# Where the degree sums of a graph kernel are made, and how far the weighing of values lags behind the scores

## The chip, the core and the metric

One Trainium2 chip, of which the kernel uses one core. The metric is the device time of one execution in microseconds (us); it was 10797.06 us, the median of three runs between 10793.86 and 10804.12. The core has five engines with a queue of instructions each, which each works through in order: TensorE (PE, matrix products), VectorE (DVE), ScalarE (ACT), GpSimdE (POOL) and SyncE (SP, which issues the DMA transfers here). They wait for each other by semaphores.

## What is computed

Four graph layers on 3327 nodes with 128 features and a dense 0/1 adjacency matrix `adj` of 3327 x 3327. Each layer takes `h = relu(layernorm(x))` and adds its result to `x`. Two of the layers matter here. Layer 1 is attention with the adjacency matrix as a bias on every score; it has 128 small heads of width 8 and takes most of the time:

```
q = (x @ Wq.T).reshape(d, n, h)          # d = 128 heads, n = 3327 nodes, h = 8
k = (x @ Wk.T).reshape(d, n, h)
v = (x @ Wv.T).reshape(d, n, h)
a = einsum('dnh,dmh->dnm', q, k) * scale
a = softmax(a + adj + adj, axis=2)
out = einsum('dnm,dmh->dnh', a, v)
```

Layer 3 needs the degree of every node, `jnp.sum(A, axis=-1)`, for its scaling by `1/sqrt(degree)`.

## The kernel before

**Stages.** Layer 0 and the projections of layer 1 take the first 416 us. Then comes the attention, to about 10070 us, and then the end: the output projection of layer 1 and layers 2 and 3. Up to the end of the attention the instructions stand on each engine in the order in which the program writes them (`manual_schedule`); nothing reorders them.

**Loops of the attention.** The 3327 queries are cut into seven chunks of 476 (`q_chunks`, the last of 471). Within a chunk the 128 heads are taken in 32 groups of four, and within a group the 3327 keys in 26 key tiles of 128. Key tiles are handled in blocks: in chunk 0 a block is a pair of key tiles (`PAIRS`, 13 blocks to a group), in chunks 1 to 6 mostly three (`TRIPLES`). For every key tile and head there are 128 x 476 scores. They come in two ways:

- *early* scores: PE multiplies keys by queries into a PSUM bank (L911, tile `early`), DVE adds the adjacency tile on the way to SBUF (L927, tile `p_early`), and when the whole block has been added, ACT takes one exp of all of it (L932). In chunk 0 a block has five early heads: the four of its first tile and one of its second. Each is a product and an add of its own, into single banks of which there are four (`bufs=4`).
- *late* scores, three heads of the block's last tile: PE puts them into one three-bank PSUM tile of which there is a single one (`late`), for one or two of the heads adds the adjacency with a product by `two_i` (L940), ACT takes the exp from PSUM (L941, tile `p_late`), and POOL multiplies the others by the exp of the adjacency (L943).

**Weighing.** Once a key tile's exps are there, PE weighs the values with them: four fp32 products per key tile (eight passes in the trace), one per head, into the bank `acc` (L954), which sums over the 26 key tiles of the group. After the last of them DVE copies `acc` to SBUF (L963, tile `o`, named `o4` in the code) and four DMAs store it (`ot`). The next group's first weighing starts a new sum in the same bank, so it waits for that copy. Tile sets of `p_early` and `p_late` come from a pool with four buffers, so block N takes the memory of block N-4.

**Order on PE in chunk 0.** For each block PE's instructions stand in the order "aAWlcW": `a` and `A` are the products of the four early heads of the first tile, `W` the weighing of one key tile, `l` the late products, `c` the fifth early product, and `W` the weighing of another key tile. The text calls the two weighings W1 and W2. DVE's adds stand in the order of their products: four for `a` and `A`, one for `c`. Which key tile is weighed follows from `ahead`: a `W` is carried out when

```
if n_tiles + heads / 2 >= n_weighed + ahead:
    weigh_next()
```

holds, where `n_tiles` counts the key tiles of the blocks begun before and `heads` the early heads of this block so far. Every second key tile, DVE also makes a pair of keys contiguous (`key_pair`, L656); at tile 5 of a group POOL does it (L658).

**Degree sums.** The adjacency tiles of a chunk are doubled and scaled by POOL (L285) and added up over the key tiles into `deg_half`, 128 partitions x 476 (L296), the last of them at key tile 17 of the chunk's group 0. What is left is the sum over the partitions. `store_sum` (L298) makes it: PE multiplies a column of ones by `deg_half` into one row of a PSUM bank, DVE scales that row to SBUF (L301), and a DMA stores it to `degd` (L302). For chunk 0 this is done among the projections (`r == 1`). For chunks 1 to 6 it is done in group 1 at key tile 10, in the PSUM tile `late` and the SBUF tile `o4`. Before layer 2 the sums are read back from `degd` into `deg`.

Of the kernel before, what the change touches and what calls it, by code (L numbers as in the profile page):

```python
# [8 lines left out]
F32 = mybir.dt.float32  # L9
# [11 lines left out]
P = 128  # L21
N = 3327
D = 128
T = 26
# [19 lines left out]
def chunks(width, size):  # L44
    return [(a, min(size, width - a)) for a in range(0, width, size)]
# [11 lines left out]
def kernel(  # L57
# [75 lines left out]
    def inv_sqrt(pool, src, name, scale=1.0, bias=0.0):  # L133
        r = pool.tile([P, T], F32, name=name)
        nc.scalar.activation(r, src, AF.Sqrt, bias=bias, scale=scale)
        nc.vector.reciprocal(r, r)
        return r
# [157 lines left out]
        else:  # L295
            nc.gpsimd.tensor_tensor(deg_half[:, :w], deg_half[:, :w], a2[:, :w], op=ALU.add)  # L296

    def store_sum(c, dp, row):  # L298
        q0, w = q_chunks[c]
        nc.tensor.matmul(dp[:1, :w], ones, deg_half[:, :w], start=True, stop=True)  # L300
        nc.vector.tensor_scalar_mul(row[:1, :w], dp[:1, :w], 0.5 / S_SCALE)  # L301
        nc.sync.dma_start(degd[:, q0 : q0 + w], row[:1, :w])  # L302

    def node_quad(agg, ps, y, t0, n, scale=1.0):
        mp = ps.tile([P, 4, D], F32, name="mp")
# [476 lines left out]
    for r in range(T):  # L782
        project_rows(r, hT4[r // 4][:, r % 4, : rows_of(r)], w_st, st, ps)
        c = r // 4 + 1
        if c < len(CS):
            if r % 4 < 2:
                norm(c, r % 4)
            if r % 4 == 2:
                norm(c, 2)
        if 2 + r < len(CS):  # L790
            more_rows(2 + r)
        if 3 + r == len(CS):
            ctx_0.close()
            kq = ctx_at.enter_context(tc.tile_pool(name="at_kq", bufs=2))
            e_pool = ctx_at.enter_context(tc.tile_pool(name="at_e", bufs=T // 2 + 1))
            kq0 = ctx_at.enter_context(tc.tile_pool(name="at_kq0", bufs=1))
            side = ctx_st.enter_context(tc.tile_pool(name="l1_side", bufs=1, side="right"))
            low_rows = []
            row = side.tile([P, 1], I32, name="row")
            nc.gpsimd.iota(row, pattern=[[0, 1]], base=0, channel_multiplier=1)  # L800
            for bit in (1, 2):
                odd = side.tile([P, 1], I32, name=f"odd{bit}")
                nc.vector.tensor_scalar(odd, row, bit, None, op0=ALU.bitwise_and)
                low = side.tile([P, 1], F32, name=f"low{bit}")
                nc.vector.tensor_scalar(low, odd, -1.0 / bit, None, op0=ALU.mult)
                low_rows.append(low)
            low_k, low_q = low_rows
        if 3 + r >= len(CS):
            while len(early) > n_early * (T - 1 - r) // (T + 3 - len(CS)):
                early.pop(0)()  # L810
        if r % 2 and r // 2 < len(CS):
            store_x(r // 2)
        if r == 1:
            store_sum(0, ps.tile([P, 512], F32, name="tp"), l1.tile([1, QW], F32, name="deg_row", bufs=1))
            nc.sync.dma_start(degd[:, N:], ones[:1])

    mx = side.tile([P, 5], F32, name="mx")
    for i, m in enumerate((q_max, k_max, a_max, low_bits, x_max)):
# [38 lines left out]
    with tc.tile_pool(name="at_in", bufs=1) as a_pool, tc.tile_pool(name="at_p", bufs=4) as p_pool, tc.tile_pool(  # L857
# [38 lines left out]
        class Block:  # L896
# [48 lines left out]
            def weigh(self, pos):  # L945
                t = self.t0 + pos
                q0, w = q_chunks[self.c]
                kp = rows_of(t)
                for i in range(4):
                    if pos < self.n - 1:  # L950
                        p = self.early[:, 4 * pos + i]
                    else:
                        p = self.late[:, i] if i < 3 else self.early[:, 4 * pos]
                    nc.tensor.matmul(  # L954
                        acc[32 * i : 32 * i + EA, :w],
                        self.v4[:kp, i, t, :],
                        p[:kp, :w],
                        start=(t == 0),
                        stop=(t == T - 1),
                    )  # L960
                if t == T - 1:
                    o4 = a_pool.tile([P, QW], F32, name="o4")
                    nc.vector.tensor_copy(o4[: 96 + EA, :w], acc[: 96 + EA, :w])  # L963
                    for i in range(4):
                        n0 = (4 * self.g + i) * N + q0
                        nc.sync.dma_start(ot[:, n0 : n0 + w], o4[32 * i : 32 * i + EA, :w])

        with tc.manual_schedule(engines=engines), ExitStack() as ctx_ps:
# [21 lines left out]
            def events(c, g, t, n, a_in):  # L990
                nonlocal coming, part, ahead_part, n_stored, k_next
                more = n < len(groups)
                if t == 8 and more:
                    coming = first[n] if n < len(first) else load_rest(*groups[n])
                if c == 0:
                    if t == 0:
                        part = ahead_part
                    part.at(t)
                    if t == 20 and g + 1 < n_groups:
                        ahead_part = Parting((g + 3) % n_groups)  # L1000
                        ahead_part.load(0)
                if t == 17:
                    while to_sum:
                        add_to_sum(*to_sum.pop(0))
                if t == 10 and g == 1 and c:
                    store_sum(c, ps.tile([P, 3, 512], F32, name="late")[:, 0], a_pool.tile([P, QW], F32, name="o4"))
                if t % 2 and n_stored < len(pairs):
                    store_tile_keys(n_stored)
                    n_stored += 1
                if t % 2 and len(pairs) < n_pairs:  # L1010
                    key_pair(nc.gpsimd if t == 5 else nc.vector, k_ins, pairs)
                if t == 14 and n + 1 < n_groups:
                    k_ins.append(load_keys(groups[n + 1][1]))
                if t == 4 and n_groups <= n < len(groups):
                    k_next = load_tile_keys(groups[n][1])
                if t == 6 and c + 1 < len(q_chunks):
                    for _ in range(min(len(to_store), 1 + T // n_groups)):
                        store_adj(*to_store.pop(0))
                    a_in += [load_adj(c + 1, i) for i in range(len(a_next), T * (g + 1) // n_groups)]
                if t == T - 4 and c + 1 < len(q_chunks):  # L1020
                    for a, i, w in a_in:
                        a_next.append(doubled(adj_pools[(c + 1) % 2], a[: rows_of(i), :w], i, w))
                        to_sum.append((a_next[-1], c + 1, i == 0))
                        to_store.append((c + 1, i, a_next[-1]))

            coming = part = None
            for n, (c, g) in enumerate(groups, 1):
# [10 lines left out]
                for i, size in enumerate(TRIPLES if c else PAIRS):  # L1038
                    if c:
                        n_g, keys, order = 3, (lambda t, k=k_now: k[:, t]), ORDERS[size, n_block % 2]  # L1040
                    else:
                        n_g, order = 1 if t0 + 1 in PARTING_TILES else 2, PAIR_ORDER
                        keys = lambda t, g=g: pairs[(g * T + t) // 2][:, t % 2]
                    block = Block(c, g, t0, size, i, q4, v4, a_t, e_t[i], n_g, keys)
                    to_weigh += [(block, pos) for pos in range(size)]
                    ahead = 7 if c else 6
                    heads = 0
                    for step in order:
                        if step == "W":
                            if n_tiles + heads / 2 >= n_weighed + ahead:  # L1050
                                weigh_next()
                        elif step == "l":
                            block.late_ones()
                        else:
                            pos, which = PIECES[step] if step != "c" else (size - 1, (3,))
                            heads += len(which)
                            block.sums(pos, which, c > 0)
                    n_tiles += size
                    n_block += 1
                    for t in range(t0, t0 + size):  # L1060
                        events(c, g, t, n, a_in)
                    t0 += size
                    if g == n_groups - 1 and c + 1 < len(q_chunks):
                        while len(e_next) < len(late_tiles) and late_tiles[len(e_next)] < t0:
                            e_next.append(exp_of(a_next[late_tiles[len(e_next)]], c + 1))
# [72 lines left out]
    def tail(general):  # L1138
# [13 lines left out]
        with ExitStack() as s:  # L1152
# [30 lines left out]

            if not general:
                nc.sync.dma_start(deg, degd.rearrange("o (p t) -> (o p) t", t=T))
            d1 = inv_sqrt(pool, deg, "d1")
            d1_in, d1_out = d1, d1
            if not general:
# [399 lines left out]
```

## Time and profile before

| | |
|---|---|
| median of three runs | 10797.06 us |
| the profiled execution, its own time | 10795.13 us |
| its span in the profile | 10793.2 us |
| granted clock of PE, mean | 0.988 |
| busy: PE, DVE, ACT, POOL | 91%, 93%, 92%, 68% |
| copies of `acc` from 416 to 1892 us (chunk 0 and the first of chunk 1) | 33, the first at 476.8, the last at 1890.3 us |
| matrix product, keys by queries, 476 columns (L911) | 367 ns |
| one pass of the weighing (L954) | 566 ns |
| DVE add of one head in chunk 0 (L927, 128 x 476) | 643 ns |
| ACT exp of a pair's early scores (L932, 128 x 2380) | 2365 ns |

The durations of one instruction overlap with the next one's: adds that follow each other start 0.56 us apart. So the text reads the time of a step from the starts in the timeline and takes a duration only where something waits for its end. In the timeline a row is: start, us taken, engine, line, operation, tiles, shapes, how many were merged, and in brackets the idle time before it with what ended it. The page's "granted clock" is the share of PE's full clock that it was given in a stretch.

### The profile page before, as it was taken

How to read it: one execution, taken by the hardware profiler on the slowest of the kernel's cores; microseconds unless marked ns; L12 is line 12 of the kernel's file. 1: busy time of each engine (PE TensorE's matmuls, PEld its weight loads, DVE VectorE, ACT ScalarE, POOL GpSimd, SP SyncE). 2: the span in 40 equal slices, each digit the busy share in tenths (PEclk: the TensorE clock that was granted, in tenths of full speed). 3: DMA queues.
4: the chain of work that ended last, by engine and by line, in shares of the span. 5: the costliest groups of instructions: out<-in, count | busy, mean ns of one | idle time of the engine just before them, and what ended most of it. 6: DMA issues, size and time to landing. Idle time of an engine off the chain costs nothing. (4 is left out here: it accounts for less than half of the span.)

```text
span 10793.2 us, 183718 instructions
## 1 busy us (share of the span) xinstructions
PE 9771.8 (91%) x74212; PEld 2128.9 (20%) x74212; DVE 10091.4 (93%) x11605; ACT 9945.0 (92%) x4716; POOL 7295.1 (68%) x3314
## 2 busy tenths in 40 slices
PE   7899999999989999899999899998999989999896
PEld 3211111111111111111111111111111111111453
DVE  6799999999999999999999999999999999999666
ACT  2799999999999999999999999999999999999432
POOL 3388887777777777777777777777777766666203
PEclk9999999999999999999999999999999999999998
DMA  8644443111111111111111111111111111111422
GB/s 300 202 101 102 101 101 86 44 44 44 44 44 42 45 44 44 43 44 46 42 45 45 42 41 45 46 42 45 42 44 44 44 37 37 38 36 37 159 95 101
DMA packets 459189, 709.21 MB, mean 66 GB/s; under 512 B 53128, under 2 KB 387967, under 8 KB 452698
## 3 DMA queue, kind: packets, MB, share of 16 engines
q1 hardware_dynamic: 455144, 690.86, 21.7%
q8 instruction: 585, 9.58, 0.4%
q0 software_dynamic: 3184, 6.51, 0.2%
q14 instruction: 276, 2.26, 0.1%
HBM read 557.43 MB, written 139.73 MB: 65 GB/s over the span
## 5 line engine op out<-in xcount | busy, mean ns | idle before, releaser
L927 DVE TENSOR_TENSOR p_early<-early,a 128x952 f32<-128x952 f32 (+3 forms) x10336 | 9152.4, 956 | 207.6 <-PE early L911 178.5
L943 POOL TENSOR_TENSOR p_late<-p_late,e 128x1428 f32<-128x1428 f32 (+3 forms) x2144 | 6397.5, 2984 | 2570.9 <-ACT p_late L941 2556.0
L932 ACT ACTIVATE p_early<-p_early 128x4284 f32<-128x4284 f32 (+3 forms) x2144 | 8077.5, 3767 | 14.7 <-DVE p_early L927 14.7
L954 PE MATMUL acc<-p_early,v 128*9 128x476 f32 (+3 forms) x33728 | 5709.9, 566 | 153.6 <-issue 110.1
L941 ACT ACTIVATE p_late<-late 128x1428 f32<-128x1428 f32 (+1 forms) x2144 | 3865.4, 1803 | 43.9 <-PE late L911 17.2
L911 PE MATMUL early<-q,k_in 32*128 32x476 f16 (+1 forms) x14784 | 3060.5, 367 | 439.1 <-DVE p_early L927 416.2
L954 PE MATMUL acc<-p_late,v 128*9 128x476 f32 (+3 forms) x12864 | 2104.0, 566 | 0.3 <-POOL p_late L943 0.3
L911 PEld LDWEIGHTS <-k_in 32*128 32x128 f16 x19968 | 765.3, 91 | 5461.1 <-issue 5440.9
L911 PE MATMUL late<-q,k_in 32*128 32x476 f16 (+1 forms) x5184 | 779.0, 367 | 179.3 <-ACT p_late L941 179.1
L954 PEld LDWEIGHTS acc<-p_early,v 128*9 128x9 f32 (+1 forms) x33728 | 655.7, 88 | 1145.6 <-issue 966.8
L911 PE MATMUL early<-q,k 32*128 32x476 f16 x2080 | 389.0, 368 | 7.5 <-DVE p_early L927 6.0
L954 PEld LDWEIGHTS acc<-p_late,v 128*9 128x9 f32 (+1 forms) x12864 | 240.7, 88 | 533.1 <-issue 438.8
L911 PEld LDWEIGHTS <-k 32*128 32x128 f16 x3328 | 120.8, 91 | 784.9 <-issue 767.3
L235 PE MATMUL agg_ps<-a,part 128*128 128x512 bf16 (+1 forms) x1092 | 229.5, 371 | 4.2 <-ACT agg L1372 3.2
L656 DVE TENSOR_REDUCE k<-k_in 128x256 f16<-128x256 f16 x377 | 220.8, 586 | 0.0
L285 POOL TENSOR_SCALAR a<-a_in 128x476 bf16<-128x476 f32 (+2 forms) x156 | 219.0, 1404 | 0.5
L348 PE MATMUL agg_ps<-a,part 128*128 128x494 bf16 (+5 forms) x728 | 168.2, 390 | 54.2 <-DMA a<-in_adjT_dram 53.3
L587 POOL TENSOR_TENSOR lo<-raw,hi 96x278 f16<-96x278 f32 (+1 forms) x256 | 182.4, 713 | 20.5
L296 POOL TENSOR_TENSOR deg_half<-deg_half,a 128x476 f32<-128x476 f32 (+1 forms) x175 | 191.9, 1097 | 2.1
L194 ACT ACTIVATE agg<-agg_ps 128x512 f32<-128x512 f32 x9 | 4.7, 597 | 196.3 <-PE agg_ps L235 196.3
L940 PE MATMUL late<-a,two_i 128*128 128x476 bf16 x544 | 182.2, 373 | 0.0
L1367 PE MATMUL sp<-yT,hT 128*128 128x512 f32 (+1 forms) x364 | 171.3, 612 | 11.6 <-ACT agg L1372 5.7
(288 smaller groups left out, 2682.1 us busy)
## 6 DMA issues: line engine op xcount, KB each, us to landing
k_in<-keyd SPq DMA_DIRECT2D x192, 832.0 KB
v<-vd SPq DMA_DIRECT2D x896, 117.0 KB
a<-in_adjT_dram SPq DMA_DIRECT2D x39, 1663.5 KB
a<-adj SPq DMA_DIRECT2D x78, 831.8 KB
a_in<-in_adjT_dram SPq DMA_DIRECT2D x125, 238.0 KB
keyd<-k SPq DMA_DIRECT2D x416, 64.0 KB
k_in<-kt SPq DMA_DIRECT2D x240, 104.0 KB
q<-qt SPq DMA_DIRECT2D x1520, 14.9 KB
```

What stands on the lines that cost most here:

```text
L235: nc.tensor.matmul(acc[c][:, :w], part[:, t, :], a[:, c0 : c0 + w], start=(t == 0 and i == 0), stop=(t == T - 1 and i == len(parts) - 1),)
L285: nc.gpsimd.tensor_scalar(a2[:kp, :w], a, 2.0 * S_SCALE, None, op0=ALU.mult)
L296: nc.gpsimd.tensor_tensor(deg_half[:, :w], deg_half[:, :w], a2[:, :w], op=ALU.add)
L587: nc.gpsimd.tensor_sub(self.lo[side][:, p], raw, hi)
L656: nc.vector.tensor_reduce(k, src.unsqueeze(3), AX.X, ALU.max)
L911: return nc.tensor.matmul(sp[:, : self.we], self.keys(self.t0 + pos)[r], self.q4[r, : self.we], start=True, stop=stop)
L927: Block.first_sum = nc.vector.tensor_tensor(p, scores, a2, op=ALU.add)
L932: nc.scalar.activation(p, p, AF.Exp, scale=1.0 / S_SCALE)
L940: nc.tensor.matmul(late[:, i, :we], two_i, self.a[pos][:, :we], start=False, stop=True)
L941: nc.scalar.activation(self.late[:, :, :we], late[:, :, :we], AF.Exp, scale=1.0 / S_SCALE)
L943: nc.gpsimd.tensor_tensor(g, g, self.e[:, :we].unsqueeze(1).to_broadcast([P, self.n_g, we]), op=ALU.mult)
L954: nc.tensor.matmul(acc[32 * i : 32 * i + EA, :w], self.v4[:kp, i, t, :], p[:kp, :w], start=(t == 0), stop=(t == T - 1),)
```

## The change

It has two parts.

First, the sums over the partitions no longer go into one row. `deg_half` becomes the stationary side, 96 columns at a time, and the ones the moving side, so that each product gives a column of 96 sums. Five columns hold a chunk's sums, and they go into the columns of `acc` behind its 476. They are made in group 0 of chunks 1 to 6, after the last weighing of the group and before the copy of `acc`, which takes them along; two more DMAs store them to `degd`, element by element. For chunk 0 the same is done in a bank among the projections. The scaling by `0.5 / S_SCALE` is done once at the end on `deg`, and the node that does not exist gets a zero there and a one added afterwards.

Second, in chunk 0 `ahead` is 8 instead of 6. At the start of a block the weighing stands seven key tiles behind instead of five: W1 of block N weighs the second tile of block N-4 (before, of block N-3), and W2 the first tile of block N-3 (before, of block N-2). The copy of `acc` moves from the third block of the next group to the fourth. Chunks 1 to 6 keep their 7.

```diff
-    def store_sum(c, dp, row):
+    SUM_ROWS = 96
+
+    def sum_columns(c, acc):
+        w = q_chunks[c][1]
+        parts = chunks(w, SUM_ROWS)
+        for j, (m0, n) in enumerate(parts):
+            nc.tensor.matmul(acc[:n, QW + j : QW + j + 1], deg_half[:, m0 : m0 + n], ones, start=True, stop=True)
+        return QW + len(parts)
+
+    def store_sums(c, o):
         q0, w = q_chunks[c]
-        nc.tensor.matmul(dp[:1, :w], ones, deg_half[:, :w], start=True, stop=True)
-        nc.vector.tensor_scalar_mul(row[:1, :w], dp[:1, :w], 0.5 / S_SCALE)
-        nc.sync.dma_start(degd[:, q0 : q0 + w], row[:1, :w])
+        whole = w // SUM_ROWS
+        nc.sync.dma_start(dram(degd, q0, [[1, SUM_ROWS], [SUM_ROWS, whole]]), o[:SUM_ROWS, QW : QW + whole])
+        if w % SUM_ROWS:
+            nc.sync.dma_start(dram(degd, q0 + whole * SUM_ROWS, [[1, w % SUM_ROWS], [1, 1]]), o[: w % SUM_ROWS, QW + whole : QW + whole + 1])
...
         if r == 1:
-            store_sum(0, ps.tile([P, 512], F32, name="tp"), l1.tile([1, QW], F32, name="deg_row", bufs=1))
-            nc.sync.dma_start(degd[:, N:], ones[:1])
+            dp = ps.tile([P, 512], F32, name="tp")
+            end = sum_columns(0, dp)
+            sums = l1.tile([P, 512], F32, name="deg_sums", bufs=1)
+            for n, c0, c1 in ((SUM_ROWS, QW, end - 1), (QW % SUM_ROWS, end - 1, end)):
+                nc.vector.tensor_copy(sums[:n, c0:c1], dp[:n, c0:c1])
+            store_sums(0, sums)
+            nc.sync.dma_start(degd[:, N:], zero[:1, :1])
...
                 if t == T - 1:
-                    o4 = a_pool.tile([P, QW], F32, name="o4")
-                    nc.vector.tensor_copy(o4[: 96 + EA, :w], acc[: 96 + EA, :w])
+                    o4 = a_pool.tile([P, 512], F32, name="o4")
+                    sums = self.c and self.g == 0
+                    end = sum_columns(self.c, acc) if sums else w
+                    nc.vector.tensor_copy(o4[: 96 + EA, :end], acc[: 96 + EA, :end])
+                    if sums:
+                        store_sums(self.c, o4)
...
-                if t == 10 and g == 1 and c:
-                    store_sum(c, ps.tile([P, 3, 512], F32, name="late")[:, 0], a_pool.tile([P, QW], F32, name="o4"))
...
-                    ahead = 7 if c else 6
+                    ahead = 7 if c else 8
...
             if not general:
                 nc.sync.dma_start(deg, degd.rearrange("o (p t) -> (o p) t", t=T))
+                nc.vector.tensor_scalar_mul(deg, deg, 0.5 / S_SCALE)
+                nc.vector.tensor_add(deg[:, T - 1 : T], deg[:, T - 1 : T], last_row)
```

## The prediction

> **What bounds the kernel now.** First the page: one long stretch in which PE, DVE and ACT are all nearly full.
>
> ```profile
> PE 9771.8 (91%) x74212; PEld 2128.9 (20%) x74212; DVE 10091.4 (93%) x11605; ACT 9945.0 (92%) x4716; POOL 7295.1 (68%) x3314
> ```
>
> Then busy time by stage (columns: us, then PE, PEld, DVE, ACT, POOL busy, granted clock), a piece of chunk 0 and most of chunks 1 to 6.
>
> ```profile
> 700.00:900.00 200.00, 195.29 (x1495) 37.00 (x1495) 195.98 (x355) 196.95 (x119) 162.03 (x153) 1.00 0.43 103
> 3300.00:10070.00 6770.00, 6154.82 (x49357) 1124.56 (x49360) 6621.37 (x6961) 6750.94 (x2884) 4867.22 (x1694) 1.00 0.14 42
> ```
>
> From chunk 1 on ACT is the bound (6750.94 of 6770). In chunk 0 PE, DVE and ACT each miss 2% or less, so a delay to any of them is paid. The waits of 500 to 1830 us name what they miss:
>
> ```profile
> PE acc L954 <- DVE o L963: 33.5, 30, 1.1
> DVE p_early L927 <- PE early L911: 29.3, 35, 1.2
> ```
>
> Both occur once per group, and the timeline, DVE then PE, shows why:
>
> ```profile
> 1004.68 2.32 DVE L927 TENSOR_TENSOR p_early<-early,a 128x476 f32<-128x476 f32 x4
> 1006.92 0.64 DVE L963 COPY o<-acc 105x476 f32<-105x476 f32 x1
> 1007.48 0.64 DVE L927 TENSOR_TENSOR p_early<-early,a 128x476 f32<-128x476 f32 x1
> 1009.01 2.90 DVE L927 TENSOR_TENSOR p_early<-early,a 128x476 f32<-128x476 f32 x5 [0.89 <-PE early L911]
> 1012.33 2.89 DVE L927 TENSOR_TENSOR p_early<-early,a 128x476 f32<-128x476 f32 x5
> ```
>
> ```profile
> 1007.62 0.98 PE L954 MATMUL acc<-p_early,v 128*9 128x476 f32 x8 [1.11 <-DVE o L963]
> 1008.54 0.38 PE L911 MATMUL early<-q,k 32*128 32x476 f16 x4
> 1008.85 0.58 PE L954 MATMUL acc<-p_late,v 128*9 128x476 f32 x3
> 1009.25 0.58 PE L954 MATMUL acc<-p_late,v 128*9 128x476 f32 x3
> ```
>
> The next group's first weighing waits for the copy of acc. Otherwise DVE runs without a gap, five adds and a key reduction per block: 1012.33 - 1009.01 = 3.32 us. A group lasts (1890.3 - 476.8) / 32 = 44.17 us, which is 13 x 3.32 and about 1.0 for the copy.
>
> **Part 1, the sum leaves the late bank.** Six times, in group 1 of chunks 1 to 6, store_sum asks for the one late bank while ACT still owes an exp from it:
>
> ```profile
> 3277.33 1.74 PE L300 MATMUL late<-deg_half,ones 128*1 128x476 f32 x2 [2.49 <-ACT p_late L941]
> 3279.11 0.64 DVE L301 TENSOR_SCALAR o<-late 1x476 f32<-1x476 f32 x1 [3.06 <-PE late L300]
> 3285.07 1.36 ACT L941 ACTIVATE p_late<-late 128x1428 f32<-128x1428 f32 x1 [4.13 <-PE late L911]
> 3287.13 3.77 ACT L932 ACTIVATE p_early<-p_early 128x4284 f32<-128x4284 f32 x1 [0.70 <-DVE p_early L927]
> ```
>
> ACT, the bound there, loses 4.13 + 0.70 = 4.8 us; the waits of ACT over chunks 1 to 6 sum to 16.8 + 7.9 + 5.3 = 30.0 us, nearly all from these six places. All of it goes: -30 (27 to 33). What is late next is nothing new, since the other groups run the same steps without it.
>
> In its place PE gets five fp32 matmuls between the last weighing and the copy, and the copy and the adds queued behind it on DVE wait for them, then the next group's first weighing. Weights of 96 columns with one moving column do not occur in the trace. The nearest row, the output projection L1180 (128 x 128 fp32), starts a pass each 0.11 us; two passes each make 10 x 0.11 = 1.1 us. Bounds: 10 x 0.088 (the weighing's loads) = 0.9, and loads and matmuls not overlapped, 10 x (0.19 + 0.28) = 4.7. In group 1 of chunk 2 the copy (3267.44) starts 0.4 us after the weighing has ended, and ACT starts its exp (3267.29) 0.8 us after the adds it needs are done (3266.47), so some 1.2 us is covered: cost about 0 per chunk, at worst 3.5, 0 to 21 in all; I take +1. The copy's five more columns are 1% of 0.64 us. The two stores of 4-byte elements stand on SP ahead of the ot stores, which waited for the same copy anyway; the copy that waits for o4 again is 42 us away: nothing. POOL's last addition to deg_half is issued some 14 key tiles before PE reads it: nothing. In the projection one 0.63 us copy becomes two small ones, under loads; before the end two tiny DVE operations (0.23 and 0.15 us by L1129 and L1121) add 0.4.
>
> [...]
>
> **Part 2, the longer lag.** At the top of block N the changed kernel has weighed up to tile 2N-8, so W1 of block N weighs tile 2N-7, the odd tile of block N-4. But p_early has four buffers: block N's adds write over block N-4's tile. The order of the two built programs (no times in it) shows what becomes of that, DVE's five adds of a block before and after:
>
> ```
> TensorTensor p_early<-early,a 128x476 [waits PE,Activation]
> TensorTensor p_early<-early,a 128x476 [waits PE] x3
> TensorTensor p_early<-early,a 128x476 [waits PE]
> ...
> TensorTensor p_early<-early,a 128x476 [waits PE,Activation]
> TensorTensor p_early<-early,a 128x476 x3
> TensorTensor p_early<-early,a 128x476 [waits PE]
> ```
>
> The first add now waits for a PE count that the last matmul of its own block's W1 sets, behind all four products, so the next three need no wait. This holds for 412 of 416 blocks. Behind it on DVE stand the three adds, the copy, the fifth add and the key reduction. And W1 stands in PE's queue behind the block's fourth product, which needs the bank that the previous block's fifth add frees (four single banks). So the engines take turns:
>
> fifth add ends, PE starts the fourth product: 0.06 (copy ends 1007.56, weighing starts 1007.62); to W1: 1008.85 - 1008.54 = 0.31; to W1's end: 1009.25 + 0.58 - 1008.85 = 0.98; PE's end to DVE: 1009.01 - 1008.92 = 0.09. Together 1.44; five adds 2.90; block 4.34 instead of 3.32. The key reduction (0.58) hides in the 1.44; ACT (3.32 of work) gets idle. That is 412 x 1.02 = +420 us.
>
> Corrections. Copy block: DVE starts 0.09 after W1, four adds 2.24 and the copy 0.64 end at 2.97, W2 from 3.03 for 0.92, the products 0.31, W1 0.98: 5.24, 0.90 over 4.34 against 1.0 now: -2. The last group's nine exps for chunk 1 (0.49 us each; its copies are 47.4 us apart) hide in ACT's idle time: -3. Start-up waits of DVE (1.3 + 1.9 us near 432 and 437) cover the first blocks: -3. The 2 tiles weighed in chunk 1 instead lie in PE's slack there: 0 (-2 to +2).
>
> The clock is the uncertain one. In the copy block, counted from W1's end, PE's fifth product follows the first add (0.09 + 0.64 + 0.06 = 0.79) and ends 0.38 later, and PE idles from 1.17 to 3.03, 1.86 us. The trace has shorter and longer waits:
>
> ```profile
> 3276.39:3283.22 6.83, 5.89 (x21) 0.54 (x21) 2.38 (x3) 4.55 (x2) 3.23 (x1) 0.50 0.27 75
> 1000.00:1013.00 13.00, 11.88 (x96) 2.10 (x88) 12.11 (x23) 12.38 (x9) 8.62 (x6) 1.00 0.18 51
> ```
>
> After the 2.49 us wait the clock is 0.50 for 6.83 us; after 1.11 it stays 1.00. 1.86 lies between. If it falls for half of the groups and half of the 2.2 us of PE work behind the copy runs at half speed, that is 0.5 x 1.2 x 32 = +20 (0 to 60). [...]
>
> **Sum** against the profiled 10795.1 (span 10793.2, 1.9 around it; the median is 1.9 higher): 420 - 2 - 3 - 3 + 20 - 30 + 1 + 0.4 = +403: 11198, and about 11200 for the median.
>
> **Rivals.** (a) Faster: the wait costs nothing, because W1 would be done before DVE has finished its key reduction, at most 0.5 us after the fifth add. For it: PE has slack in most blocks. Against: fourth product and W1 alone take 1.29 us after that add. It would leave -30 and at most -6 of the copy's stall, which moves to a block in which PE has one more product to do and DVE no key reduction before it: 10761 to 10768. (b) PE stays at the low clock through chunk 0: its work of 3.07 us per block (0.31 + 0.92 + 0.62 + 0.30 + 0.92) takes some 1.8 times as long, 5.5 (passes of the weighing 0.76 apart from 3281.72 on, 0.40 at 1008.85): 412 x 2.2 - 30 = +876, 11670. For it: the granted clock is 0.58 on average from 416 to 436.5 us, where chunk 0 starts. Against: at 0.50 PE has no gap, and from 436.5 on, after a stretch without gaps, it is 1.00. (c) The sums cost as much as the late bank did (+21 of the bound): the total changes by 20 only, inside the range.
>
> **How the numbers follow.** Forecast 0.86, (a) 0.06, (b) 0.06, else 0.02. Ends: a block's extra time 0.93 to 1.10 (latencies 0.08 either way), clock 0 to 60, sums 0 to 21, late bank 27 to 33: from 383 - 8 - 33 = +342 (11140) to 453 - 5 + 60 - 27 + 21 = +502 (11300); I go 20 below for waits partly hidden: 11120 to 11300. A change under 0.2% (22 us) could not be told from none: faster 0.06, same 0.01, slower 0.93.
>
> **What would show it.** Right: chunk 0 blocks 4.3 us apart, DVE waiting at L927 about 0.9 us per block for PE acc or early, copies 56 to 58 us apart; no L301, and chunks 1 to 6 some 5 us shorter each. Wrong: DVE without gaps in chunk 0 (then a), or a granted clock near 0.5 between 440 and 2200 us (then b), or new ACT idle time behind the first copies of chunks 1 to 6 (then c).

## The result, and the profile after

The changed kernel takes 11216.83 us, the median of six runs (11213.46 to 11220.40), against 10798.46 us for the kernel before in the same comparison (six runs, 10793.86 to 10805.82): 1.0386 times as long, interval 1.0373 to 1.0400. The profiled execution took 11213.46 us, span 11211.8, 418.3 us more than the profiled execution before.

Line numbers have moved: the add of the early scores is now L942 (was L927), the early product L926 (L911), the weighing L969 (L954), the copy of `acc` L980 (L963), the exp of the early scores L947 (L932), the sums matmuls L304, the key reduction L666 (L656).

The page's engine line: busy time is little changed, only the span has grown.

```profile
PE 10020.4 (89%) x74268; PEld 2178.8 (19%) x74268; DVE 10119.1 (90%) x11602; ACT 9987.4 (89%) x4716; POOL 7299.3 (65%) x3314
```

DVE's busy time has grown by 28 us and ACT's by 42, in a span that is 418 us longer. Busy time by stage (us, then PE, PEld, DVE, ACT, POOL, granted clock), for the same two pieces as before:

```profile
700.00:900.00 200.00, 174.26 (x1137) 32.18 (x1137) 153.08 (x271) 155.57 (x90) 122.21 (x109) 0.99 0.29 73
3300.00:10070.00 6770.00, 6160.28 (x49441) 1132.61 (x49435) 6629.73 (x6968) 6762.70 (x2896) 4893.75 (x1704) 1.00 0.15 43
```

In chunk 0 no engine is full any more: DVE went from 195.98 of 200 us to 153.08, ACT from 196.95 to 155.57. From chunk 1 on, ACT is fuller than before (6762.70 of 6770, was 6750.94). The waits of 500 to 2230 us name the new one (us in total, times, longest):

```profile
DVE p_early L942 <- PE acc L969: 410.4, 388, 2.9
ACT p_early L947 <- DVE p_early L942: 366.3, 388, 1.4
PE acc L969 <- DVE o L980: 54.7, 29, 1.9
```

Nearly every block of chunk 0 has it once, 410.4 / 388 = 1.06 us each. The timeline, DVE and then PE, shows one turn of the loop:

```profile
1005.21 2.90 DVE L942 TENSOR_TENSOR p_early<-early,a 128x476 f32<-128x476 f32 x5 [0.96 <-PE acc L969]
1008.02 0.59 DVE L666 TENSOR_REDUCE k<-k_in 128x256 f16<-128x256 f16 x1
1009.57 2.89 DVE L942 TENSOR_TENSOR p_early<-early,a 128x476 f32<-128x476 f32 x5 [0.96 <-PE acc L969]
```

```profile
1008.16 0.36 PE L926 MATMUL early<-q,k 32*128 32x476 f16 x1 [0.19 <-DVE p_early L942]
1008.44 0.58 PE L969 MATMUL acc<-p_late,v 128*9 128x476 f32 x3
...
1008.87 0.56 PE L969 MATMUL acc<-p_early,v 128*9 128x476 f32 x1
```

The fifth add ends at 1008.11 (1005.21 + 2.90), PE starts the fourth product at 1008.16, W1 at 1008.44, W1 ends at 1009.43 (1008.87 + 0.56), and DVE begins the next block's adds at 1009.57. One block lasts 1009.57 - 1005.21 = 4.36 us; DVE stands still while PE makes the fourth product and W1, and PE's fourth product waits until DVE has ended the fifth add.

The starts of the first copy of `acc` in each chunk, and of the last copy, cut the 418 us into stages:

| stage | before, us | after, us | difference |
|---|---|---|---|
| to the first copy of chunk 1 | 1890.31 | 2333.64 | +443.3 |
| chunk 1 (to the first copy of chunk 2) | 1377.13 | 1371.22 | -5.9 |
| chunks 2, 3, 4, 5 | 1374.04, 1373.79, 1373.99, 1373.37 | 1368.31, 1369.41, 1368.19, 1368.70 | -5.7, -4.4, -5.8, -4.7 |
| chunk 6 (to the last copy) | 1312.72 | 1313.03 | +0.3 |
| after it | 717.8 | 719.2 | +1.4 |

So chunk 0 lost, chunks 1 to 5 gained, and chunk 6, which was to gain as well, did not.

### The profile page after: what moved, and what is told of

Its sections match the earlier page's. It is cut to its first block, busy times and chain, and to the rows that moved or that the text cites. A ratio compares the mean times of both kernels' runs of the same rounds, so it can differ in the third digit from the quotient of the medians.

```text
span 11211.8 us, 183829 instructions
## 1 busy us (share of the span) xinstructions
PE 10020.4 (89%) x74268; PEld 2178.8 (19%) x74268; DVE 10119.1 (90%) x11602; ACT 9987.4 (89%) x4716; POOL 7299.3 (65%) x3314
## 5 line engine op out<-in xcount | busy, mean ns | idle before, releaser
L942 DVE TENSOR_TENSOR p_early<-early,a 128x952 f32<-128x952 f32 (+3 forms) x10336 | 9152.4, 956 | 603.6 <-PE acc L969 440.6
L947 ACT ACTIVATE p_early<-p_early 128x4284 f32<-128x4284 f32 (+3 forms) x2144 | 8125.9, 3790 | 393.4 <-DVE p_early L942 393.3
L969 PE MATMUL acc<-p_early,v 128*9 128x476 f32 (+3 forms) x33728 | 5717.4, 566 | 178.0 <-issue 112.2
L956 ACT ACTIVATE p_late<-late 128x1428 f32<-128x1428 f32 (+1 forms) x2144 | 3907.9, 1823 | 36.9 <-PE late L955 26.0
L926 PE MATMUL early<-q,k_in 32*128 32x476 f16 (+1 forms) x14784 | 3060.7, 367 | 437.5 <-DVE p_early L942 411.3
L969 PE MATMUL acc<-p_late,v 128*9 128x476 f32 (+3 forms) x12864 | 2105.5, 566 | 0.2 <-POOL p_late L958 0.2
L926 PEld LDWEIGHTS <-k_in 32*128 32x128 f16 x19968 | 767.4, 91 | 5444.1 <-issue 5423.9
L926 PE MATMUL late<-q,k_in 32*128 32x476 f16 (+1 forms) x5184 | 778.7, 368 | 180.3 <-ACT p_late L956 180.1
L969 PEld LDWEIGHTS acc<-p_early,v 128*9 128x9 f32 (+1 forms) x33728 | 657.6, 88 | 1261.6 <-issue 1058.0
L926 PE MATMUL early<-q,k 32*128 32x476 f16 x2080 | 587.7, 370 | 187.7 <-DVE p_early L942 142.8
L969 PEld LDWEIGHTS acc<-p_late,v 128*9 128x9 f32 (+1 forms) x12864 | 241.2, 88 | 662.9 <-issue 567.5
L926 PEld LDWEIGHTS <-k 32*128 32x128 f16 x3328 | 156.1, 91 | 940.5 <-issue 491.7
L666 DVE TENSOR_REDUCE k<-k_in 128x256 f16<-128x256 f16 x377 | 223.0, 592 | 0.0
```

Of the source, the lines that this page charges most:

```text
L666: nc.vector.tensor_reduce(k, src.unsqueeze(3), AX.X, ALU.max)
L926: return nc.tensor.matmul(sp[:, : self.we], self.keys(self.t0 + pos)[r], self.q4[r, : self.we], start=True, stop=stop)
L942: Block.first_sum = nc.vector.tensor_tensor(p, scores, a2, op=ALU.add)
L947: nc.scalar.activation(p, p, AF.Exp, scale=1.0 / S_SCALE)
L956: nc.scalar.activation(self.late[:, :, :we], late[:, :, :we], AF.Exp, scale=1.0 / S_SCALE)
L969: nc.tensor.matmul(acc[32 * i : 32 * i + EA, :w], self.v4[:kp, i, t, :], p[:kp, :w], start=(t == 0), stop=(t == T - 1),)
```

## Experiments

"Lag" is the value of `ahead` in chunk 0: 6 before, 8 after. "A group" is the time from one copy of `acc` to the next in chunk 0.

**Lag 6, the new sums alone.**

```diff
-                    ahead = 7 if c else 8
+                    ahead = 7 if c else 6
```

> Part 1 alone: sums in the spare columns, lag in chunk 0 as before the change. If the whole slowdown comes from the wait of a block's first add for its own W1 (theory A), chunk 0 has groups of 44.1 us again and what is left is the saving that the changed kernel shows in chunks 1 to 6 (5.9 + 5.7 + 4.4 + 5.8 + 4.7 - 0.3 = 26 us): about 10772. If the sums' matmuls or scattered stores carry part of it (theory B), it is at or above the kernel before, 10798 or more.

Measured: 10786.66 us (11 runs, 10777.82 to 10792.25), 0.9986 of before (0.9977 to 0.9995). Chunk 0's groups are back at 44.1 us, so all of the loss comes from the lag. The gain of the sums is 11 us and not 25, so the size that theory A gave is not met, though the loss is gone. Its profiled execution (10789.89 us, slower than the median) shows where much of the gain went: the attention began 11.5 us later than before, chunks 1 to 5 gave 6.3, 2.1, 3.8, 5.3 and 5.2 us, and chunk 6 lost 0.6. In chunks 2 and 3 the granted clock fell to one half 2.6 and 2.8 us behind the first copy, for 6.8 and 3.4 us; the group that follows lasts 45.83 and 44.36 us, against 42.84 in chunks 4 and 5, and ACT waits for PE once, 2.0 and 0.7 us. Chunk 6 and the start are taken up below.

**Lag 8 alone, the sums as before.** In the kernel before:

```diff
-                    ahead = 7 if c else 6
+                    ahead = 7 if c else 8
```

> Part 2 alone: the kernel before with the lag of the changed kernel in chunk 0. Theory A: chunk 0 as in the changed kernel (groups of 57.6 and 58.9 us, blocks of 4.35), the late-bank stalls of chunks 1 to 6 are back: 11217 + 26 = 11243. Theory B (the two parts hurt only together): clearly less than 11217.

Measured: 11238.57 us (one run). Groups are 57.6 us as in the changed kernel. So lag 8 makes the wait with either way of making the sums. It costs 441 us with the old row and, against the run with lag 6, 430 with the columns.

**Five buffers for chunk 0's exps, lag 8.**

```diff
+            p_pools = [ctx_ps0.enter_context(tc.tile_pool(name="at_p0", bufs=5))]
...
-                self.early = p_pool.tile([P, 9, QW], F32, name="p_early")
-                self.late = p_pool.tile([P, 3, QW], F32, name="p_late")
+                self.early = p_pools[-1].tile([P, 9 if c else 5, QW], F32, name="p_early")
+                self.late = p_pools[-1].tile([P, 3, QW], F32, name="p_late")
...
+                            while to_weigh:
+                                weigh_next()
...
+                            p_pools.append(ctx_ps.enter_context(tc.tile_pool(name="at_p", bufs=4)))
```

> The changed kernel, lag 8 kept, but p_early and p_late of chunk 0 have five buffers of their own instead of four; all pending weighings are done before chunk 1 begins, which adds some 8 us once. Theory A: the wait for W1 goes, groups of at most 44.1 us (43.9 by the working of rival a): 10772 - 6 + 8 = 10774 (10760 to 10790). Theory C: groups stay near 57.6 us, 11200 or more.

Measured: 10780.41 us (10 runs, 10775.31 to 10787.67), 0.9983 of before (0.9974 to 0.9993); groups of 43.93 us. In its waits of 500 to 1860 us (the add is L940 here, the product L924, the weighing L967, the copy L978) the add waits for W1 no more; what is left is a wait for its product, and PE's for the copy:

```profile
DVE p_early L940 <- PE early L924: 25.2, 72, 1.1
PE acc L967 <- DVE o L978: 23.3, 30, 1.1
```

**The same with four buffers**, to see that the fifth buffer did it and not the new pool or the flush of the weighings before chunk 1:

```diff
-            p_pools = [ctx_ps0.enter_context(tc.tile_pool(name="at_p0", bufs=5))]
+            p_pools = [ctx_ps0.enter_context(tc.tile_pool(name="at_p0", bufs=4))]
```

> The kernel with five buffers for p_early in chunk 0, but with four: chunk 0's own pool of a and p_early and the flush of weighings ahead of chunk 1 stay, only the fifth buffer goes. Theory A (the number of buffers against the lag is what makes the wait): groups of chunk 0 are again 57.6 us against 43.9 with five, the time about 11222 us. Rival B (the separate pool or the flush took the wait away): about 10780 us.

Measured: 11221.17 us (one run), groups of 57.58 us where the clock does not fall, and the wait stands where it stood (500 to 2230 us):

```profile
DVE p_early L940 <- PE acc L967: 410.8, 388, 2.9
```

The number of buffers against the lag is the cause, shown from both sides: with one buffer more 436 us are gone, with a lag shorter by one 458, by two 430.

**Lag 7.** W2 of block N-1 then weighs the last tile of block N-4, ahead of all of block N in PE's queue.

```diff
-                    ahead = 7 if c else 8
+                    ahead = 7
```

> The changed kernel with a lag that is one key tile shorter (ahead 7): W1 of block N then weighs the first tile of block N-3 and W2 its second, so block N-4's buffer is free before block N begins. Theory A: no wait for W1, DVE without gaps, groups of at most 44.1 us; and as the copy now stands a W, a block's first four products and a W apart from the next sum, its stall falls from 1.1 to some 0.4 us: 43.5 per group, 10772 - 18 = 10754 (10745 to 10775). Theory C (a longer lag is itself what costs, for whatever reason): about halfway, near 10990.

Measured: 10758.93 us (10754.13 to 10764.74), 0.9964 of before (0.9951 to 0.9978); groups of 43.38 us, 0.74 less than the 44.12 before. With lag 7 the last weighing of a group is a W2 and the next group's first is the W1 of the following block, so four early products stand between them, while the copy is made. The waits of 500 to 1860 us, where the kernel before had 33.5 us (30 times) and 29.3 us (35 times):

```profile
PE acc L969 <- DVE o L980: 6.6, 30, 0.2
DVE p_early L942 <- PE early L926: 7.2, 14, 1.2
```

This is the edge: with a lag of one key tile more the group is 14 us longer.

**Chunk 0's copies of `acc` on ACT, lag 8 and four buffers.**

```diff
-                    nc.vector.tensor_copy(o4[: 96 + EA, :end], acc[: 96 + EA, :end])
+                    (nc.vector.tensor_copy if self.c else nc.scalar.copy)(o4[: 96 + EA, :end], acc[: 96 + EA, :end])
```

> The changed kernel (lag 8, four buffers) with chunk 0's copies of the accumulator into o4 made by ACT instead of DVE; no change in the waits of the adds. Theory A (the copy is 0.6 us in DVE's queue between a block's adds, it makes TensorE idle 1.86 us once in a group, and only that idle time takes the granted clock to 0.5 in every third group): the groups fall from 57.58 to about 56.6 us, the clock stays at 1.00 through chunk 0, and the time is 11217 - 31 x 0.97 - 13.5 = about 11173 us. Rival B (TensorE's 1 us waits in every block are enough to lower the clock by chance of position): every third group still takes 1.3 us more, about 11187 us. Rival C (ACT's copy delays its exps and the chain runs through them): 11217 us or more.

Measured: 11182.69 us (11176.71 to 11189.01), 1.0359 of before (1.0343 to 1.0375). Groups are 56.64 us, as A said, and the granted clock stays up: ten falls in chunk 0 of the changed kernel, in the steady groups here none. The total gives only 34 of the 44 us that A expected. Over the first 30 intervals the trace gives 40.6; the last two, at the change to chunk 1, take 5.4 back (55.93 and 44.62 us, were 52.90 and 42.26). There the last copy of chunk 0 stands on ACT behind the exp of a block of chunk 1 (3.77 us, from 2250.88) and starts at 2254.54 us. PE waits 3.90 us for it, the granted clock falls to one half for 6.83 us, and ACT waits 5.04 us for the next late scores. That is rival C, in this one place.

**The scaling of the sums in the moving column, lag 7.** Chunk 6 first, in the changed kernel: DVE's timeline in its second group.

```profile
9179.47 0.66 DVE L980 COPY o<-acc 105x481 f32<-105x481 f32 x1 [0.47 <-PE acc L304]
9180.04 6.37 DVE L942 TENSOR_TENSOR p_early<-early,a 128x944 f32<-128x944 f32 x6
9190.87 1.05 DVE L1203 TENSOR_SCALAR deg<-deg 128x26 f32<-128x26 f32 x1 [4.46 <-DMA deg<-degd]
```

The scaling of `deg` is written behind the attention, but the last sums are stored right after chunk 6's first copy, and the instruction stands there, among the adds. DVE waits 4.46 us for the load of `degd`, and the adds stand behind it. The load itself is late because it must follow the scattered stores: SyncE waits 5.6 us for them before it issues it, where it waited 1.3 us for the row in the kernel before. The waits of 9175 to 9200 us show PE and ACT stopped with DVE:

```profile
PE early L926 <- DVE p_early L942: 5.9, 3, 5.1
ACT p_early L947 <- DVE p_early L942: 5.2, 2, 5.0
DVE deg L1203 <- DMA deg<-degd: 4.5, 1, 4.5
```

The experiment removes both operations on `deg`; the ones in the matmul carry the factor.

```diff
-            nc.tensor.matmul(acc[:n, QW + j : QW + j + 1], deg_half[:, m0 : m0 + n], ones, start=True, stop=True)
+            nc.tensor.matmul(acc[:n, QW + j : QW + j + 1], deg_half[:, m0 : m0 + n], scaled_one, start=True, stop=True)
...
-            nc.sync.dma_start(degd[:, N:], zero[:1, :1])
+            nc.sync.dma_start(degd[:, N:], ones[:1])
...
-                nc.vector.tensor_scalar_mul(deg, deg, 0.5 / S_SCALE)
-                nc.vector.tensor_add(deg[:, T - 1 : T], deg[:, T - 1 : T], last_row)
```

> Lag 7 in chunk 0, and the scaling by 0.5/S_SCALE is put into the moving column of the sums matmuls, so that the two operations on deg no longer stand in DVE's queue behind the load of deg. Theory A (the missing saving of chunk 6 is the 4.5 us that DVE waits for degd in that chunk and the 1.05 us operation behind it): chunk 6's first interval from copy to copy falls from 49.3 to about 43 us, 10758.9 - 5.5 = about 10753 us, chunks 0 to 5 as in the run with lag 7 alone. Rival B (the 49.3 us interval has another cause, such as the load of deg itself or the last chunk's other work): interval and time unchanged, 10757 to 10761 us.

Measured: 10750.20 us (10741.45 to 10758.04), 0.9956 of before (0.9942 to 0.9969). Of the two rivals A holds in the trace: the interval in which DVE had waited, from chunk 6's first copy to its second, was 49.31 us with lag 7 alone and became 42.52, and the whole of chunk 6 is 6.9 us shorter (1313.24 to 1306.35). DVE's adds (L944 here) behind the copy (L982) have no break any more:

```profile
8720.27 0.66 DVE L982 COPY o<-acc 105x481 f32<-105x481 f32 x1 [0.47 <-PE acc L306]
8720.84 16.92 DVE L944 TENSOR_TENSOR p_early<-early,a 128x944 f32<-128x944 f32 x17
```

The medians differ by 8.7 us, with runs that overlap. It is the fastest of the versions that keep the new sums throughout.

**The old row among the projections, lag 7 and scaled column.**

```diff
-            end = sum_columns(0, dp)
-            sums = l1.tile([P, 512], F32, name="deg_sums", bufs=1)
-            for n, c0, c1 in ((SUM_ROWS, QW, end - 1), (QW % SUM_ROWS, end - 1, end)):
-                nc.vector.tensor_copy(sums[:n, c0:c1], dp[:n, c0:c1])
-            store_sums(0, sums)
+            row = l1.tile([1, QW], F32, name="deg_row", bufs=1)
+            nc.tensor.matmul(dp[:1, :QW], ones, deg_half[:, :QW], start=True, stop=True)
+            nc.vector.tensor_scalar_mul(row, dp[:1, :QW], 0.5 / S_SCALE)
+            nc.sync.dma_start(degd[:, :QW], row)
```

> The kernel with lag 7 and the scaled column, but with chunk 0's sums made in the projections as before the change: one matmul with 476 columns, one scaled row, one store of 1.9 KB. Theory A (the two scattered stores and the two small copies among the projections are what puts attention's start 3 us later): the first add of chunk 0 starts at about 421.8 us as in the kernel before, not at 424.8 to 425.1 us, and the time is about 3 us below the run with the scaled column alone, some 10750 us. Rival B (the start's delay comes from elsewhere): first add at 424 us or later, time within 1 us of that run.

Measured: 10748.73 us (10742.56 to 10755.99), 0.9957 of before (0.9944 to 0.9971): 1.5 us below the run with the columns, less than the spread of either, so the time tells nothing. The trace does. The first add is at 419.61 us (426.55 with the columns). More than half of that difference (3.8 of 6.9 us) is older than the sums: the kernels reach the sums matmuls anywhere from 253 to 264 us, in no order that follows the edits. The rest comes after them. From the start of the sums matmuls to the start of the last maximum of the projections it is 159.44, 158.83 and 158.94 us in the three kernels with the old row, and 161.8 to 162.6 in six of seven with the columns. The seventh, with five buffers, has 159.9.

**A plain store in place of chunk 0's scattered stores**, with the products and copies left in. The row that is stored is a constant, so this kernel leaves out chunk 0's real degrees:

```diff
-            store_sums(0, sums)
+            row = l1.tile([1, QW], F32, name="deg_row", bufs=1)
+            nc.vector.memset(row, 2.0)
+            nc.sync.dma_start(degd[:, :QW], row)
```

> The kernel with lag 7 and the scaled column; the five column products and the two small copies among the projections stay, but chunk 0's two scattered stores are left out, and a constant row of 1.9 KB is stored in their place (chunk 0's degrees are not the real ones). Measured from the start of the sums matmuls to the start of the last maximum of the projections (q_max or k_max): 159.4, 158.8 and 158.9 us in the three runs with the old row, 161.8 to 162.6 us in six of the seven runs with the columns so far (159.9 in one). Theory A (the scattered stores hold the DMA engines for some 3 us in a stage that they bound): about 159 us. Rival B (the products, the copies or the tile deg_sums cost it): about 162 us.

Measured: 10752.38 us (one run), and 160.73 us to the last maximum, between the two. The way there is clearer. The 11th maximum after the sums comes 40.7 us after them here, 40.7 to 41.0 with the old row and 41.5 to 42.1 with the scattered stores; the 29th after 101.77 us here, 101.3 to 101.9 with the old row and 104.2 to 105.1 with the scattered stores (102.5 with five buffers). Up to there the stores account for all of it. From there to the last maximum it takes 59.0 us, where the kernels above take 57.4 to 57.8. The kernel with the stores twice, below, takes 58.9 there as well, so the scattered stores are not the cause of that 1.4 us, which stays open. The four microseconds that follow some 6.5 us after the sums, in the changed kernel and in this one (last two columns: DMA share, GB/s):

```profile
262.00:266.00 4.00, 4.00 (x20) 2.52 (x19) 2.24 (x3) 1.99 (x3) 0.68 (x1) 1.00 1.31 65
```

```profile
269.40:273.40 4.00, 4.00 (x20) 2.49 (x19) 2.34 (x3) 1.89 (x3) 0.58 (x1) 1.00 1.06 317
```

The DMA engines are full in both (a packet's whole time is counted where it starts, so a share can pass 1), but behind the scattered stores of 1.9 KB they move 65 GB/s instead of 317. The same stretch has 318 and 320 GB/s in two kernels with the old row, and 66 with the scaled column. By an estimate from these two rows 4 x (1 - 65/317) = 3.2 us of transfers are put off, in a stage that the transfers bound: from 300 to 416 us the DMA share is 0.97 in the kernel before.

**The scattered stores twice.**

```diff
             store_sums(0, sums)
+            store_sums(0, sums)
```

> The kernel with lag 7 and the scaled column, with chunk 0's two scattered stores issued twice. From the start of the sums matmuls to the start of the last maximum: theory A (each pair of scattered stores costs the projections some 3 us of DMA time) about 165 us, between 164 and 166; rival B (the stores are hidden and something else costs it) about 162 us.

Measured: 10759.27 us (one run), 167.83 us to the last maximum, above A's 164 to 166, and not a clean doubling. The second pair writes where the first does, and SyncE waited for that, with the projections' transfers behind it (SP's waits, 256 to 270 us):

```profile
SPq L312 <- DMA degd<-deg_sums: 6.3, 1, 6.3
```

It shows a wait of 6.3 us for scattered stores to land, but not the price of one that nobody waits for. Neither theory foresaw this wait.

## Why the prediction was right, and where its sum was off

**The wait of the longer lag** came as described: the first add of a block stands behind its own block's W1, the copies are 57 to 59 us apart, and five buffers or a lag of 7 take it away. A block was summed to 4.34 us and lasts 4.36; in the copy block PE's idle time was summed to 1.86 and is 1.89. A steady group lasts 57.58 us against 44.12, so 32 x 13.46 = 431 us, where the sum had 418. The miss is 0.03 us per block, 416 times. (One of the sum's corrections is off in itself: 0.90 instead of 1.0 in 32 groups is -3 us, not -2.)

**The clock** fell less often than assumed. PE's weighing behind the copy shows the idle stretch of 1.89 us in two groups; in the first its eight passes take 1.78 us instead of 0.98:

```profile
1136.37 1.78 PE L969 MATMUL acc<-p_early,v 128*9 128x476 f32 x8 [1.89 <-DVE o L980]
1078.79 0.98 PE L969 MATMUL acc<-p_early,v 128*9 128x476 f32 x8 [1.89 <-DVE o L980]
```

The granted clock (third column from the end) in stretches of 3.41 us, laid so that the fall from 1136.00 to 1139.41 us fills one of them, the first group in four rows, the second in the last two:

```profile
1129.18:1132.59 3.41, 2.89 (x21) 0.59 (x22) 2.78 (x5) 2.49 (x3) 1.38 (x1) 1.00 0.01 3
1132.59:1136.00 3.41, 1.87 (x14) 0.30 (x6) 2.58 (x5) 2.97 (x2) 1.77 (x3) 0.99 0.00 0
1136.00:1139.41 3.41, 3.04 (x20) 0.36 (x20) 1.39 (x3) 2.19 (x1) 2.98 (x5) 0.51 0.26 63
1139.41:1142.83 3.42, 3.28 (x25) 0.61 (x18) 2.75 (x5) 1.36 (x1) 0.55 (x1) 1.00 0.39 102
1074.57:1077.98 3.41, 2.31 (x15) 0.42 (x14) 2.13 (x4) 3.41 (x2) 1.86 (x2) 1.00 0.01 2
1077.98:1081.39 3.41, 2.60 (x24) 0.55 (x25) 2.08 (x5) 2.00 (x1) 3.17 (x5) 1.00 0.20 50
```

In these two groups the clock went to one half for 3.41 us where most of that idle time lay in a single one of the stretches (PE busy 1.87 of 3.41), and stayed where it was split over two (2.31 and 2.60). That makes no rule: with lag 8 alone the clock stayed at 1.00 after a stretch with PE busy 1.77 of 3.41 (1017.12 to 1020.53 us), and in the changed kernel it fell to 0.50 at the start of chunk 1 after one with 3.27 (2330.64 to 2334.06 us). Ten of 31 groups were hit, with 1.35 us each: 13.5 us, where the sum had 20 for half of the groups. That the two are near is partly luck, since no row told in which groups the clock would fall.

**The late bank** was worth what the sum said, 30 (27 to 33). With the scaling gone from DVE's queue the time from chunk 1's first copy to the last falls from 8185.1 to 8152.5 us, by 32.6, in the kernel with the scaled column, and by 26.9 to 34.6 in the three built on it. In the changed kernel only 26.2 of it arrived.

**The mis-sized term** is the one for the two tiny operations on `deg`: "before the end two tiny DVE operations (0.23 and 0.15 us by L1129 and L1121) add 0.4". Their place was read from the source. In the order of instructions on DVE they stand in chunk 6, behind a load. There they cost 6.9 us: the 4.5 us wait, 1.05 us for the scaling, and the rest behind them; the granted clock falls there too, for 6.8 us. With it chunk 6 lost what the late bank had given it.

**The scattered store** was booked at nothing twice, "which waited for the same copy anyway" in the attention and "under loads" among the projections. The first holds in chunks 1 to 5 of the changed kernel: ACT's waits there come to 1.4 us, where they were 24.6, and the sums matmuls are ten passes 0.085 us apart, less than the 0.11 taken. It does not hold in chunk 6, where the load of `degd` waited for the stores. The second does not hold. In the projections the transfers are what bounds (DMA share 0.97 from 300 to 416 us before), and the attention's first add comes 2.7 us later, counted from the sums (169.38 us, was 166.66). The prediction had taken it that nothing waits for these stores. What waits is the next transfer, and in chunk 6 the load. What makes such a store slow the traces do not show.

Together: 443.3 - 26.2 + 1.4 = 418.5 us by the stages, against 403 in the sum. Some 13 us of the miss is the group, 7 us the scaling in chunk 6, 3 us the stores in the projections; the clock took 6.5 back, and chunks 1 to 6 without the scaling some 4. So the total came out within 16 us in part because misses of both signs met.

**The rivals.** (a), a hidden wait, was ruled out by the gaps of 0.96 us in every block. (b), a clock that stays low, by the mean clock of 0.99 in chunk 0. (c), sums as dear as the late bank, by DVE's wait for the sums in the changed kernel, 0.47 us. Yet its sign, ACT idle behind a chunk's first copy, does come in three of the other kernels: in chunks 2 and 3 with lag 6, 2 and 4 with the old row among the projections, 2 with the stores twice. Each time the granted clock falls 2.5 to 2.9 us behind that copy, the group lasts 44.4 to 45.8 us instead of 42.85, and ACT waits 0.7 to 2.4 us. The sums stand just before the fall; whether they cause it was not tested. Such falls and the start, which differs by some 10 us between the kernels, hide a term of a few microseconds in the total.

**Left open:** what the late start of the run with lag 6 comes from: 8.8 of the 11.5 us lie before the sums (263.9 us in its profile, 255.1 before), and whether that differs by the execution alone isn't known. Open too is what decides whether the clock falls.

## What to carry to other kernels

A consumer may lag behind its producer only so far that the writer finds its memory free. Here four buffers hold eight key tiles: a lag of 7 costs nothing, a lag of 8 costs 1.06 us in nearly every block, and with a fifth buffer it costs nothing again. Count it in the order of the queue: which instruction frees the buffer, and does it stand before or behind what the writer of that buffer must deliver first. Look up every small operation in the order of the engine's queue, not in the source, and ask what load it waits for; and ask what transfers stand behind a store of single elements: among the projections, where the transfers bound (DMA share 0.97), 1.9 KB of it cost some 3 us (2.7 by the first add, 3.2 by the estimate from 65 and 317 GB/s).

## What the runs showed of the hardware that was not expected

- Behind stores of 4-byte elements, 1.9 KB in all, the DMA engines moved 65 GB/s for 4 us at a busy share of 1.31, against 317 GB/s at 1.06 behind a plain store.
- After the same idle time of 1.89 us the granted clock of TensorE fell to 0.51 for 3.41 us in one group of the changed kernel (PE busy 1.87 of the 3.41 us before it) and stayed at 1.00 in another (2.31 and 2.60 of 3.41 in the two stretches that share the idle time); with lag 8 alone it also stayed at 1.77. In the steady groups of the kernel with ACT's copy it did not fall at all: there the idle stretch before the copy block's weighing was 0.25 us.
- SyncE waited 5.6 us for two scattered stores before it issued a load of the same memory, 1.3 us for a plain row in the kernel before; DVE waited 4.46 us for that load in the middle of the attention.
